# A graph network's GRU gates by block products: the state's side of the candidate as seven products, Silu as one function

## The chip, the cores and the metric

The kernel runs on one core of a Trainium2 chip. The metric is the time on the device in microseconds (us), the median of several runs. Everything is computed in fp32.

Five engines work side by side, each through its own instructions in order: TensorE (PE, with its weight loads shown as PEld), VectorE (DVE), ScalarE (ACT), GpSimd (POOL), and SyncE (SP), which issues DMA transfers. They wait for each other through semaphores. [...]

## The reference, cut to what matters

There are 128 graphs of 64 nodes with 256 features, and four layers, each with a residual and a layer norm. Layer 0 is a gated graph network of five steps, and most of the work lies there:

```python
A = (adj != 0).astype(x.dtype)
h = x
for l in range(weight.shape[0]):                 # five
    m = jnp.einsum('bnd,de->bne', h, weight[l])
    agg = jnp.einsum('bij,bid->bjd', A, m)
    h = _gru_cell(agg, h, w_ih, w_hh, b_ih, b_hh)

# _gru_cell(m, h, ...):
gi = m @ w_ih.T + b_ih                           # three gates of 256 columns
gh = h @ w_hh.T + b_hh
r = jax.nn.sigmoid(i_r + h_r)
z = jax.nn.sigmoid(i_z + h_z)
n = jnp.tanh(i_n + r * h_n)                      # n: the candidate; h_n: the state's side of it
return (1.0 - z) * n + z * h
```

Layer 1 is an MLP of 256 to 1024 to 256 on the aggregated nodes, with an RMS norm and `jax.nn.silu` between its two products. Layer 2 maps to and from a hyperbolic ball (a logarithm, a tanh), and layer 3 is attention over the graph's edges (an exp).

## The kernel before

Two graphs make a block of 128 rows, four blocks a group of 512 rows, and there are 16 groups. Three groups are in flight at a time, each with its own buffers. Features lie on the partitions: the state of a group is `h[128, 2, 512]`, two halves of the features (k) by 512 nodes, and the nodes are cut into two halves (n) of 256. The message weights are multiplied into the gate weights beforehand.

The kernel doesn't issue its instructions as they are written. It first records all operations with an assumed duration, then searches for an order of each engine by a beam search over that model, and issues them in that order. An operation that ScalarE or VectorE may do is given to one of them by the search. A PSUM bank is taken by the first operation on it and comes free after the last.

Gates r and z need `[r; z] = [[W_ar, W_hr], [W_az, W_hz]] [agg; h]`, a product of 2x2 blocks if the nodes are cut in two as well. Winograd's form of Strassen's scheme does such a product with seven block products and a few sums in place of eight. A block product here is 256x256 by 256x256, four matmuls of 128x128 by 128x256:

```python
def product(ps, w, v, first, last, r):
    for c in range(KD):                          # KD = 2
        for k in range(KD):
            pe(256, lambda c=c, k=k: nc.tensor.matmul(
                ps[:, c * HR:(c + 1) * HR], w[:, k, c * P:(c + 1) * P], v(k), ...))

def sides(n):                                    # aggregate, and the state's side of the candidate
    if l:
        ps = rows_of(h, n)                       # four transposes
        copied(512, ...)
    p_agg = aggregate(agg, hr, 2 * n, n)         # four matmuls of 128 columns, and a copy
    p_hn = bank("p_hn")
    product(p_hn, w_hn, lambda k: h[:, k, half(n)], True, True, (h, n))
    for c in range(KD):
        scaled(300, lambda c=c: hnb[:, c, half(n)], lambda c=c: p_hn[:, c * HR:(c + 1) * HR], lambda: 0.5, ...)
    return p_agg
# ... (cut)
sides(0)
product(p1, a11[l], k_of(a, 0), True, False, (a, 0))
copied(420, lambda: uu.tile(), lambda: blocks_of(p1.tile()), [uu], [p1])
product(p_in[0], w_in[l], k_of(a, 0), True, True, (a, 0))
product(p1, a12, k_of(h, 0), False, True, (h, 0))
tanh_half(ur, lambda c: p1[:, c * HR:(c + 1) * HR], 0, p1)
new_n(0, ur)
p_a2 = sides(1)
a2 = lambda: blocks_of(p_a2.tile())
minus(t1, a2, of(a, 0), [p_a2, (a, 0)])          # four VectorE sums of 512 columns
minus(t2, of(h, 1), lambda: view(t1), [(h, 1), t1])
minus(t3, of(h, 1), a2, [(h, 1), p_a2])
minus(t4, lambda: view(t2), of(h, 0), [t2, (h, 0)])
product(pu, s2[l], k_view(t2), True, True, t2)
plus(uu, pu, uu)
product(pv, s3[l], k_view(t3), True, False, t3)
plus(uv, pv, uu)
product(pw, s1[l], k_view(t1), True, False, t1)
product(pv, na22, k_view(t4), False, True, t4)
plus(uv, pw, uv)
plus(uz, pv, uu)
product(pw, s4[l], k_of(h, 1), False, True, (h, 1))
# ... (cut: the tanhs and the new state)
product(p_in[1], w_in[l], k_of(a, 1), True, True, (a, 1))
```

Sigmoids are computed as tanh of half the argument. The MLP's Silu is computed with tanh too, for each of eight chunks of 128 hidden features, with the missing 0.5 put into the residual and the RMS weight into `w2s` during the setup:

```python
dve(512, ... nc.vector.scalar_tensor_tensor(v, v, b1c(c), ps_r.tile(), OP.add, OP.mult) ...)
act(512, ... nc.scalar.activation(th.tile(), v, AF.Tanh, scale=half_r[:, c:c + 1]) ...)
dve(512, ... nc.vector.scalar_tensor_tensor(v, th.tile(), 1.0, v, OP.add, OP.mult) ...)
```

The MLP's first product is done in seven block products as well (`by_sums`, tiles `p_1h`, `p_uh`, `p_vh`, `p_wh`), except in the last two groups, where it is done directly (`ps_hid`). Its second product is `ps_o`.

Of the kernel before, what the change touches and what calls it, by code (L numbers as in the profile page):

```python
# [14 lines left out]
OP = mybir.AluOpType  # L15

P = 128
# [25 lines left out]
class Op:  # L43
    __slots__ = ("eng", "us", "run", "ways", "stream", "n", "kb", "need", "then", "bufs", "opens", "id", "way")

    def __init__(self, ways, stream, n, kb):
        self.ways = {eng: (us, run) for eng, us, run in ways}
        self.eng, self.us, self.run = ways[0]
        self.stream, self.n, self.kb = stream, n, kb
        self.need, self.then, self.bufs, self.opens, self.id, self.way = 0, [], (), None, 0, 0.0  # L50


class Plan:


    def __init__(self, flow):
# [10 lines left out]
        self.past, self.order = None, []  # L67

    def copy(self):
# [6 lines left out]
        c.past, c.order = (self.past, self.order), []  # L76
        return c

    def advance(self, until, rank):
# [3 lines left out]
        while self.left and clock["PE"] < until:  # L83
            best = None
            for s in range(self.first, min(self.first + flow.WINDOW, len(self.queues))):
                for e, q in self.queues[s].items():
                    opened = False
                    for _, o in zip(range(flow.AHEAD[e]), q):
# [10 lines left out]
                        key = (t + o.ways[e][0] - min(w[0] for w in o.ways.values()) if len(o.ways) > 1 else t, *rank(s, o))  # L99
# [4 lines left out]
            _, o, eng, t = best  # L104
            for e in o.ways:
                self.queues[o.stream][e].remove(o)
# [37 lines left out]
class Flow:  # L144
# [13 lines left out]
    HOPS = {"from PE": 0.25, "to PE": 0.3, "else": 0.1}  # L158
# [4 lines left out]
    WINDOW, STRETCH, WIDTH, LAG = 4, 25.0, 8, 40.0  # L163


    ENDGAME = 350.0
# [10 lines left out]
    def op(self, eng, us, run, w=(), r=(), kb=0):  # L177
        self.either([(eng, us, run)], w, r, kb)

    def either(self, ways, w, r, kb=0):  # L180

        o = Op(ways, len(self.streams) - 1, len(self.ops), kb)
# [31 lines left out]
    def hop(self, e, to):  # L214
        if e == to:
            return 0.0
# [14 lines left out]
    def issue(self):  # L231
        self.ways()
        ranks = (lambda s, o: (s, o.n), lambda s, o: (s if o.kb else -s, o.n), lambda s, o: (self.LAG * s - o.way, s, o.n))
        plans, until = [Plan(self)], 0.0
        while any(p.left for p in plans):
            late = until > self.work - self.ENDGAME
            until += self.STRETCH / 2 if late else self.STRETCH
# [6 lines left out]
            plans = [found[k] for k in sorted(found)[:self.WIDTH * (3 if late else 1)]]  # L244
# [16 lines left out]
def kernel(  # L261
# [79 lines left out]
    def dve(n, run, w, r):  # L341
        flow.op("DVE", 0.16 + 0.00105 * n, run, w, r)

    def act(n, run, w, r):
        flow.op("ACT", 0.27 + 0.00077 * n, run, w, r)

    def copied(n, o, i, w, r):

        flow.either([("ACT", 0.27 + 0.00077 * n, lambda: nc.scalar.copy(o(), i())),  # L349
                     ("DVE", 0.16 + 0.00105 * n, lambda: nc.vector.tensor_copy(o(), i()))], w, r)  # L350

    def scaled(n, o, i, scale, bias, w, r):

        flow.either([("ACT", 0.27 + 0.00077 * n, lambda: nc.scalar.activation(o(), i(), AF.Identity, bias=bias(), scale=scale())),  # L354
                     ("DVE", 0.16 + 0.00105 * n, lambda: nc.vector.tensor_scalar(o(), i(), scale(), bias(), OP.mult, OP.add))], w, r)
# [62 lines left out]
    def gate_w(name):  # L418
        return fixed([P, KD, D], name)

    a12, na22, w_hn = gate_w("a12"), gate_w("na22"), gate_w("w_hn")
    a11, s1, s2, s3, s4, w_in = ([gate_w(f"{n}_{l}") for l in range(L)] for n in ("a11", "s1", "s2", "s3", "s4", "w_in"))

# [5 lines left out]
    half_b, half_r = fixed([P, NV], "half_b"), fixed([P, KH], "half_r")  # L429
# [36 lines left out]
    flow.op("ACT", 1.5, lambda: nc.scalar.activation(warm, one4, AF.Tanh))  # L466
# [23 lines left out]
    dve(4, lambda: nc.vector.tensor_scalar(half_r.tile(), cols[:, 2 * NV + KH:], 0.5, None, OP.mult), [half_r], [cols])  # L490
# [13 lines left out]
    def hh_out(i, k, ps):  # L504
        if i == 0:
            dve(256, lambda: nc.vector.tensor_copy(a12[:, k, :], ps[:, :D]), [(a12, k)], [ps])
            dve(256, lambda: nc.vector.tensor_scalar(na22[:, k, :], ps[:, D:], -1.0, None, OP.mult), [(na22, k)], [ps])
        else:
# [594 lines left out]
```

## Time and profile before

| what | value |
|---|---|
| time, median of 3 runs | 2432.22 us (2432.07 to 2432.49) |
| span of the profiled execution | 2430.5 us |
| granted TensorE clock | 0.994 |
| bytes read from and written to HBM | 25.74 MB and 8.39 MB |

A group in the list of instructions reads: line of the kernel, engine, operation, output tile<-input tiles, shape, count; then after a bar the busy time in us and the mean duration of one in ns; then after another bar the idle time of that engine just before these instructions, with what ended it. A line can be that of a helper: all products of the GRU stand at one line and are told apart by their tiles. TensorE's records overlap, so that the busy times of its groups add up to more than its whole. A matmul of fp32 shows as two records, a transpose as one.

TensorE's waits over the whole span add up to little (engine, operation, what it waited for: us in total, times, longest):

```profile
PE ps_T L633 <- ACT x_n L354: 5.3, 1, 5.3
PE ps_sup L333 <- ACT tan L995: 3.6, 1, 3.6
PE ps_sup L333 <- DVE tan L994: 3.0, 1, 3.0
PE ps_hid L333 <- DVE aggm L350: 2.5, 1, 2.5
PE ps_x L469 <- POOL ident masks.py:199: 2.5, 1, 2.5
```

Four of these are of layers 1 to 3 of the last groups, and one is at the very start.

### The profile page before, as it was taken

What the parts mean: (1) busy time and instruction counts of PE and PEld (TensorE: products, weight loads), DVE (VectorE), ACT (ScalarE), POOL (GpSimd) and SP (SyncE); (2) the same over time, 40 slices, a digit from 0 to 9 for tenths busy, and PEclk for the clock granted to TensorE, in tenths of its full rate; (3) what the DMA queues carried; (4) which work ended last, traced back from release to release, by engine and by line L of the source; (5) the groups of instructions that cost most, each with busy time, mean ns of one, the idle gap of its engine ahead of it and who ended that gap; (6) DMA issues with size and microseconds to landing.
All of it is one profiled execution on the core that took longest, in us unless ns stands there. A gap on an engine that the chain in (4) does not pass through costs nothing.

```text
span 2430.5 us, 32703 instructions
## 1 busy us (share of the span) xinstructions
PE 2394.7 (99%) x12258; PEld 2102.9 (87%) x12258; DVE 1893.4 (78%) x4097; ACT 1147.1 (47%) x2408; POOL 188.2 (8%) x144
## 2 busy tenths in 40 slices
PE   9999999999999999999999999999999999999995
PEld 7888888888888888888888888888888888888864
DVE  3668787887888877778777887888787787878777
ACT  4434544444444444454444545455444544445453
POOL 4000000000100000000000100000000000000011
PEclk9999999999999999999999999999999999999997
DMA  4000000000000000000000000000000000000000
GB/s 127 3 1 12 1 29 1 18 12 1 29 1 27 3 18 11 1 27 3 16 14 1 29 1 27 3 19 11 1 29 1 18 12 1 27 9 18 9 9 18
DMA packets 39725, 36.21 MB, mean 15 GB/s; under 512 B 9956, under 2 KB 38656, under 8 KB 39568
## 3 DMA queue, kind: packets, MB, share of 16 engines
q1 hardware_dynamic: 37840, 32.25, 4.2%
q8 instruction: 97, 1.59, 0.3%
q10 hardware_dynamic: 1328, 1.31, 0.2%
q0 software_dynamic: 400, 0.57, 0.1%
q14 instruction: 60, 0.49, 0.1%
HBM read 25.74 MB, written 8.39 MB: 14 GB/s over the span
## 4 chain that ended last, share of the span: by engine, by line
PE 94%; DVE 4%; ACT 1%; DMA 1%; issue 0%; POOL 0%; SPq 0%; POOLq 0%; ACTq 0%; DVEq 0%
PE p_v L663 11%; PE p_w L663 11%; PE p_in L663 11%; PE p_r L663 11%; PE p_hn L663 11%; PE ps_o L333 9%; PE ps_agg L333 6%; PE p_u L663 6%; PE ps_hr L643 3%; PE ps_a L333 2%; PE p_wh L882 2%; PE p_vh L882 2%; PE p_1h L882 2%; PE ps_T L633 1%; PE ps_att L333 1%; PE p_uh L882 1%
## 5 line engine op out<-in xcount | busy, mean ns | idle before, releaser
L663 PE MATMUL p_hn<-hT,w_hn 128*128 128x256 f32 x1280 | 322.8, 380 | 0.0
L663 PE MATMUL p_in<-agg,w_in 128*128 128x256 f32 x1280 | 315.4, 379 | 0.0
L663 PEld LDWEIGHTS p_in<-agg,w_in 128*128 128x128 f32 x1280 | 240.2, 190 | 31.1
L663 PEld LDWEIGHTS p_hn<-hT,w_hn 128*128 128x128 f32 x1280 | 227.9, 191 | 22.7
L333 PE MATMUL ps_o<-w2s,hid 128*128 128x256 f32 x1024 | 231.2, 379 | 0.0
L333 PEld LDWEIGHTS ps_o<-w2s,hid 128*128 128x128 f32 x1024 | 193.9, 190 | 27.3 <-issue 1.2
L678 POOL TENSOR_TENSOR rstd<-ve,pow 128x4 f32<-128x4 f32 (+1 forms) x64 | 82.5, 1289 | 1491.6 <-DVE ve L676 1484.0
L767 ACT ACTIVATE V<-V,half_b 128x256 f32<-128x256 f32 x160 | 72.7, 500 | 199.2 <-DVE V L763 199.0
L663 PE MATMUL p_u<-tA,s 128*128 128x256 f32 x640 | 158.1, 381 | 1.4 <-DVE tA L746 0.6
L663 PE MATMUL p_w<-tA,s 128*128 128x256 f32 x640 | 158.1, 379 | 0.0
L663 PE MATMUL p_r<-hT,a 128*128 128x256 f32 x640 | 156.9, 379 | 0.0
L663 PE MATMUL p_r<-agg,a 128*128 128x256 f32 x640 | 156.7, 379 | 0.0
L663 PE MATMUL p_v<-tB,s 128*128 128x256 f32 x640 | 155.4, 379 | 0.0
L663 PE MATMUL p_v<-tB,na 128*128 128x256 f32 x640 | 154.5, 379 | 0.0
L663 PE MATMUL p_w<-hT,s 128*128 128x256 f32 x640 | 154.3, 379 | 0.0
L349 ACT COPY agg<-ps_agg 128x512 f32<-128x512 f32 x154 | 89.9, 584 | 114.2 <-PE ps_agg L333 98.8
L333 PEld LDWEIGHTS ps_agg<-edge,hr 128*128 128x128 f32 x1024 | 136.1, 191 | 6.6
L354 ACT ACTIVATE hnb<-p_hn,half_b 128x256 f32<-128x256 f32 x232 | 101.6, 472 | 81.4 <-PE p_hn L663 67.4
L333 PE MATMUL ps_agg<-edge,hr 128*128 128x128 f32 x1024 | 138.8, 275 | 0.0
L663 PEld LDWEIGHTS p_u<-tA,s 128*128 128x128 f32 x640 | 119.3, 190 | 21.0 <-DVE tA L746 2.3
L663 PEld LDWEIGHTS p_v<-tB,s 128*128 128x128 f32 x640 | 120.9, 190 | 16.3 <-PE ps_att L333 0.2
L663 PEld LDWEIGHTS p_w<-hT,s 128*128 128x128 f32 x640 | 120.7, 190 | 16.0
(233 smaller groups left out, 4686.5 us busy)
## 6 DMA issues: line engine op xcount, KB each, us to landing
x<-in_x_dram SPq DMA_DIRECT2D x16, 512.0 KB, 3.6
xr<-in_x_dram SPq DMA_DIRECT2D x16, 512.0 KB, 3.6
out_dram<-x_n SPq DMA_DIRECT2D x16, 512.0 KB, 2.9
edge<-in_adj_dram SPq DMA_DIRECT2D x32, 64.0 KB, 2.3
wm<-in_L_gnn_weight_dram SPq DMA_DIRECT2D x5, 256.0 KB, 5.3
w2s<-in_L_gnn_W_dram SPq DMA_DIRECT2D x1, 1024.0 KB, 10.0
w<-in_L_gnn_W_dram SPq DMA_DIRECT2D x2, 512.0 KB, 3.5
w_in_L_gnn_w_hh_dram<-in_L_gnn_w_hh_dram ACTq DMA_DIRECT2D x1, 512.0 KB, 5.2
```

The lines of the kernel that those rows point to most:

```text
L333: return nc.tensor.matmul(o, lhsT, rhs, start=(k == 0), stop=(k == nk - 1))
L349: flow.either([("ACT", 0.27 + 0.00077 * n, lambda: nc.scalar.copy(o(), i())), ("DVE", 0.16 + 0.00105 * n, lambda: nc.vector.tensor_copy(o( ...
L354: flow.either([("ACT", 0.27 + 0.00077 * n, lambda: nc.scalar.activation(o(), i(), AF.Identity, bias=bias(), scale=scale())), ("DVE", 0.16 ...
L633: turn(lambda j=j, c=c: nc.tensor.transpose(ps[:, c * HR + j * P:c * HR + (j + 1) * P], src[:, 2 * n + j, c * P:(c + 1) * P], ident.tile() ...
L643: turn(lambda j=j, c=c: nc.tensor.transpose(ps[:, j * D + c * P:j * D + (c + 1) * P], src[:, c, (2 * n + j) * P:(2 * n + j + 1) * P], iden ...
L663: pe(256, lambda c=c, k=k: nc.tensor.matmul(ps[:, c * HR:(c + 1) * HR], w[:, k, c * P:(c + 1) * P], v(k), start=first and c == k == 0, sto ...
L678: pool(1.1, lambda: nc.gpsimd.tensor_tensor(rstd[:, :m, :], ve[:, :m, :], pow2[:, :m, :], OP.pow), [rstd], [ve])
L767: act(256, lambda c=c: nc.scalar.activation(o[:, c, :], src(c), AF.Tanh, bias=half_b[:, i * KD + c:i * KD + c + 1], scale=0.5), [(o, c)], ...
L882: pe(256, lambda c=c: nc.tensor.matmul(ps[:, c * HR:(c + 1) * HR], w1f[:, w, (2 * q + c) * P:(2 * q + c + 1) * P], v[0](), start=first and ...
```

## The change

It has three parts that change what the engines do, and one that changes the search.

First, the gates are split in another way. The 2x2 blocks are no longer (aggregate, state) by (node halves), but (feature halves) by (node halves), once for the aggregate and once for the state. Both are summed in PSUM, so the chain of additions after the products stays one. The sums of the state (`tA`) then serve a second time.

Second, they serve the state's side of the candidate, which becomes a Winograd product of its own: seven block products of 128x128 by 128x256, one matmul each, in two banks.

Third, Silu is one ScalarE function, with the RMS weight as its scale; the second VectorE pass and the scaling of `w2s` go.

The search knows ScalarE's function tables (a change is taken to cost 1.28 us, and tanh is taken to be in the sets of both exp and silu), adds 0.4 us to VectorE's start where either engine may do an operation, has other assumed durations, and looks at more plans in smaller steps near the end. Each PSUM bank counts as one thing in it: an operation on one half of a bank comes after those before it on the other half if one of them writes.

The diff, cut to its core:

```diff
@@ the search
+                        elif o.sets and self.table not in o.sets:
+                            t += flow.TABLE
-                        key = (t + o.ways[e][0] - min(w[0] for w in o.ways.values()) if len(o.ways) > 1 else t, *rank(s, o))
+                        key = (t + flow.SOONER if len(o.ways) > 1 and e == "DVE" else t, *rank(s, o))
+    SOONER = 0.4
+    TABLE = 1.28
-    WINDOW, STRETCH, WIDTH, LAG = 4, 25.0, 8, 40.0
-    ENDGAME = 350.0
+    WINDOW, STRETCH, WIDTH, LAGS = 4, 37.5, 8, (60.0, 150.0,)
+    ENDGAME, LAST_STRETCH, LAST_WIDTH = 400.0, 10.0, 32
-            until += self.STRETCH / 2 if late else self.STRETCH
+            until += self.LAST_STRETCH if late else self.STRETCH
-            plans = [found[k] for k in sorted(found)[:self.WIDTH * (3 if late else 1)]]
+            plans = [found[k] for k in sorted(found)[:self.LAST_WIDTH if late else self.WIDTH]]
+    TANH, EXP, LN, SILU = ("exp", "silu"), ("exp",), ("ln",), ("silu",)
 ... (cut)
@@ the weights
-    a12, na22, w_hn = gate_w("a12"), gate_w("na22"), gate_w("w_hn")
-    a11, s1, s2, s3, s4, w_in = ([gate_w(f"{n}_{l}") for l in range(L)] for n in ("a11", "s1", "s2", "s3", "s4", "w_in"))
+    w_h, w_hn = fixed([P, 7, D], "w_h"), fixed([P, 7, P], "w_hn")
+    w_a, w_in = [fixed([P, 7, D], f"w_a_{l}") for l in range(L)], [fixed([P, KD, D], f"w_in_{l}") for l in range(L)]
-        sums("DVE", 0.7) if l == 0 else sums("POOL", 1.32)
+        sums_of(w_a[l], "DVE", 0.43) if l == 0 else sums_of(w_a[l], "POOL", 0.8)
-    for k in range(KH):
-        act(256, lambda k=k: nc.scalar.activation(w2s[:, k, :], w2s[:, k, :], AF.Identity, scale=rmsc(k)), [(w2s, k)], [(w2s, k), cols])
 ... (cut)
@@ the GRU
-                p_hn = bank("p_hn")
-                product(p_hn, w_hn, lambda k: h[:, k, half(n)], True, True, (h, n))
 ... (cut)
+            def sums(x, i):
 ... (cut)
+                for o, x0, x1 in ((of(t1), at(0, 1), at(0, 0)), (of(t2), at(1, 1), of(t1)),
+                                  (of(t3), at(1, 1), at(0, 1)), (of(t4), of(t2), at(1, 0))):
+                    dve(256, lambda o=o, x0=x0, x1=x1: nc.vector.tensor_sub(o[0](), x0[0](), x1[0]()),
+                        [o[1]], [x0[1], x1[1]])
 ... (cut)
+            def gate(ps, m, v, first, last):
+                for i, w in ((1, w_h), (0, w_a[l])):
+                    for c in range(KD):
+                        pe(256, lambda i=i, w=w, c=c: nc.tensor.matmul(
+                            ps[:, c * HR:(c + 1) * HR], w[:, m, c * P:(c + 1) * P], v[i][0](),
 ... (cut)
+            def state_side():
+                px, py = bank("p_hx"), bank("p_hy")
+                hs = u("hs", f"hs{l}", (P, 2, HR))
 ... (cut: prod is one matmul; plus is one VectorE addition of 256 columns out of PSUM)
+                prod(px, 0, m11, block(0, 0), True)
+                copied(256, su[0], lambda: px[:, :HR], [su[1]], [px])
+                prod(px, 0, m12, block(1, 0))
+                scaled(256, out(0, 0)[0], lambda: px[:, :HR], lambda: 1.0, lambda: b(0), [out(0, 0)[1]], [px, half_b])
+                prod(px, 1, ms2, sum_of(t2))
+                plus(su, px, 1, su)
+                prod(py, 0, ms3, sum_of(t3), True)
+                plus(sv, py, 0, su)
+                prod(py, 1, ms1, sum_of(t1))
+                prod(py, 0, mn22, sum_of(t4))
+                plus(out(0, 1), py, 0, su, 1)
+                plus(out(1, 1), py, 1, sv, 1)
+                prod(py, 1, ms4, block(1, 1))
+                plus(out(1, 0), py, 1, su, 0)
 ... (cut)
-            sides(0)
-            product(p1, a11[l], k_of(a, 0), True, False, (a, 0))
+            agg_of(0)
+            gate(p1, m11, block(0, 0), True, False)
             copied(420, lambda: uu.tile(), lambda: blocks_of(p1.tile()), [uu], [p1])
-            product(p_in[0], w_in[l], k_of(a, 0), True, True, (a, 0))
-            product(p1, a12, k_of(h, 0), False, True, (h, 0))
+            gate(p1, m12, block(1, 0), False, True)
             tanh_half(ur, lambda c: p1[:, c * HR:(c + 1) * HR], 0, p1)
+            sums(h, 1)
+            state_side()
+            product(p_in[0], w_in[l], lambda k: agg[:, k, half(0)], True, True, (agg, 0))
             new_n(0, ur)
-            p_a2 = sides(1)
 ... (cut: four minus lines go)
+            agg_of(1)
+            sums(agg, 0)
-            product(pu, s2[l], k_view(t2), True, True, t2)
+            gate(pu, ms2, sum_of(t2), True, True)
             plus(uu, pu, uu)
 ... (cut: pv, pw in the same way)
@@ the MLP's activation
-            act(512, lambda v=v, th=th, c=c: nc.scalar.activation(th.tile(), v, AF.Tanh, scale=half_r[:, c:c + 1]),
-                [th], [*parts, half_r])
-            dve(512, lambda v=v, th=th: nc.vector.scalar_tensor_tensor(
-                v, th.tile(), 1.0, v, OP.add, OP.mult), parts, [*parts, th])
+            act(512, lambda v=v, c=c: nc.scalar.activation(v, v, AF.Silu, scale=rmsc(c)), parts, [*parts, cols], SILU)
```

## The prediction

> **What bounds the kernel now.** I read the page's shares first, then TensorE's waits, then the stages, and only then the costs of single rows.
>
> ```profile
> PE 2394.7 (99%) x12258; PEld 2102.9 (87%) x12258; DVE 1893.4 (78%) x4097; ACT 1147.1 (47%) x2408; POOL 188.2 (8%) x144
> PE 94%; DVE 4%; ACT 1%; DMA 1%; issue 0%; POOL 0%; SPq 0%; POOLq 0%; ACTq 0%; DVEq 0%
> ```
>
> TensorE is busy for 2394.7 of 2430.5 us and makes up 94% of the chain that ended last; VectorE follows at 78%. [...] The stages say the same (columns: stretch, its length, then busy time and count of PE, PEld, DVE, ACT, POOL, the clock, DMA):
>
> ```profile
> 100.00:500.00 400.00, 399.53 (x2072) 354.51 (x2071) 311.21 (x640) 184.81 (x391) 19.49 (x15) 1.00 0.03 11
> 1000.00:1500.00 500.00, 500.00 (x2589) 444.50 (x2588) 401.10 (x886) 245.88 (x520) 34.84 (x24) 1.00 0.04 13
> 2300.00:2400.00 100.00, 86.38 (x350) 61.70 (x349) 77.28 (x192) 50.51 (x97) 13.86 (x9) 0.93 0.02 6
> 2400.00:2431.00 31.00, 14.61 (x64) 12.14 (x64) 22.17 (x86) 12.12 (x28) 4.72 (x4) 0.72 0.10 35
> ```
>
> In the middle TensorE stands still for nothing. Of its 35.8 us of idle time 13.6 + 16.4 = 30.0 lie after 2300 us, when the last groups run out of work for it, 3.4 in the first 30 us, and the rest, some 2.4 us, is spread over 2270 us. So one microsecond of TensorE work removed is one microsecond of time, as long as VectorE and the schedule keep up; anything removed elsewhere is worth nothing except in the last 50 us.
>
> **What one matmul costs.** Rows of the page can't be divided for this: a 128x256 fp32 product shows as two records of 379 ns that overlap with their neighbours (p_hn: 640 products in the code, x1280 in the row). I take a long unbroken run from the chain in order of time (start, length, what):
>
> ```profile
> 2363.80 15.99 PE ps_o L333 x74
> ...
> 2402.30 1.97 PE ps_T L633 x8
> ```
>
> 15.99 us / 74 records = 0.216 us for a record, 0.432 us for a product of 128x256. Check: all 256-wide records (7040 of the GRU, 1024 ps_o, 784 of the first MLP product, 552 others) make 9400 x 0.216 = 2030 us, 104 records of 512 columns make 45, and the 2754 transposes and 128-wide or narrower ones then have 320 us, 0.116 each, about half of 0.216. It closes, so there is no hidden cost for switching between streams.
>
> **The change part by part.**
>
> *Matmuls of the GRU.* Per group and layer the kernel before issues 44 products of 256 columns: 28 for the two gates r and z (p_r 8, p_u 4, p_v 8, p_w 8), 8 for p_in, 8 for the state's side p_hn (two halves x 2 x 2 blocks). After it the gates are split differently: the 2x2 blocks are no longer (aggregate, state) but the two feature halves, done once for the aggregate and once for the state, both summed in PSUM. That is 7 block products x 2 inputs x 2 output columns = 28 again. p_in keeps 8. The state's side of the candidate becomes one Winograd product of seven blocks, each one matmul: 7. So 43 in place of 44. Aggregations (8) and transposes (8) stay. Over 16 groups x 5 layers: 80 products x 0.432 = **34.6 us less for TensorE**. In the trace p_hn x1280 should become 1120 records, split over two tiles.
>
> *Sums on VectorE.* The rows before:
>
> ```profile
> L746 DVE TENSOR_TENSOR tA<-hT,tA 128x512 f32<-128x512 f32 x80 | 59.4, 742 | 1.4
> L746 DVE TENSOR_TENSOR tB<-tA,hT 128x512 f32<-128x512 f32 x80 | 57.9, 725 | 0.0
> L746 DVE TENSOR_TENSOR tA<-ps_agg,agg 128x512 f32<-128x512 f32 x80 | 54.9, 688 | 48.7 <-PE ps_agg L333 36.6 <-ACT agg L349 11.6
> L746 DVE TENSOR_TENSOR tB<-hT,ps_agg 128x512 f32<-128x512 f32 x80 | 54.5, 681 | 0.0
> L355 DVE TENSOR_SCALAR hnb<-p_hn,half_b 128x256 f32<-128x256 f32 x88 | 41.4, 480 | 19.6 <-PE p_hn L663 10.7 <-ACT hnb L354 8.5
> L878 DVE TENSOR_TENSOR t<-aggm 128x256 f32<-128x256 f32 x28 | 12.9, 462 | 1.8 <-ACT aggm L349 1.5
> L946 DVE SCALAR_TENSOR_TENSOR hid<-th,hid 128x512 f32<-128x512 f32 x128 | 82.8, 688 | 0.3 <-ACT th L944 0.2
> L354 ACT ACTIVATE hnb<-p_hn,half_b 128x256 f32<-128x256 f32 x232 | 101.6, 472 | 81.4 <-PE p_hn L663 67.4
> ```
>
> [...] Out go the four 512-wide sums, 59.4 + 57.9 + 54.9 + 54.5 = 226.7 us, the part of the scaling of p_hn that ran on VectorE, 41.4, and the second pass of the activation, 82.8: together 351. In come eight 256-wide sums for each group and layer, 640 x about 0.44 (the L878 rows, 462 down to 418 ns) = 281, and five 256-wide additions out of PSUM, 400 x 0.45 (the 128x256 operations that read PSUM lie between 420 and 484 ns) = 180. The copy and the scaling of the new chain, 160 in all, I leave mostly to ScalarE, since the new search delays VectorE by 0.4 us where either may do it; 15 us stay here, and some 20 us of other work move off by the same rule. Sum: 1893 - 351 + 281 + 180 + 15 - 20 = **about 2000 us, 83% of the span**, 85% in the middle against 80% now. [...] (0.69 to 0.74 us for 512 columns, 0.42 to 0.46 for 256, so about 0.15 of it is fixed), and that is why halving the width adds 54 us here. It stays below TensorE's 2360 and costs nothing by itself.
>
> *ScalarE.* 128 Tanh passes of 720 ns are replaced by 128 Silu passes of the same shape; I take the same duration. ScalarE loses 101.6 us of p_hn scaling and gains at most 160 x 0.45 = 72. What is new is the table: Tanh and Exp shared one table, and the only changes were to Ln and back:
>
> ```profile
> L975 ACT ACT_TABLE_LOAD x15 | 19.2, 1283 | 0.3
> L767 ACT ACT_TABLE_LOAD x10 | 12.8, 1283 | 0.2
> ```
>
> With the loads at three other lines that is 31, about two a group. [...] the change treats Silu as being in a set with tanh and without exp. Then a group needs Silu, Ln, and Exp or tanh, and with three groups mixed the order may go to and fro: I expect 45 to 65 loads, so 18 to 43 us more of ScalarE, at 47% load. Off the path, except that each holds up the operations behind it by 1.3 us.
>
> *Setup.* Eight scalings of w2s go (3.5 us of ScalarE), one half_r too; GpSimd's sums for layers 1 to 4 get smaller. TensorE does the same work there. Worth nothing, or a few tenths.
>
> *The end.* After the last ps_o, at 2379.8, there are 50.7 us of layer norm, logarithm, ball and attention. None of its operations changes; the search gets finer there (steps of 10 instead of 12.5 us, 32 plans instead of 24). I put the gain at 0 to 4 us, and a loss of 1 to 3 for an extra table load and longer layers of the last group. Net zero.
>
> *Sum.* TensorE work 2394.7 - 34.6 = 2360.1; idle time 35.8 + 2 for new short waits of TensorE in the middle = 37.8; with the 1.7 us between the profile's span and the time that is 2399.6; I take off 1.6 for the better end: **2398 us, 1.4% less**.
>
> **The rivals.**
>
> *The chain of the state's side becomes a wait.* The seven products hang together through two banks: product, eviction, product in the same bank, addition, and so on. [...] The chain is 7 x 0.43 + 7 x 0.46 = 6.2 us plus hand-overs, say 8 to 9, and it now needs both halves of the state. For it: r's candidate waits at its end, and two banks of eight are held three times as long. Against it: three groups are in flight, so each layer of a group, with some 22 us of TensorE work, has about 43 us of the other two to lie under, and the first MLP product already runs such chains (p_vh, p_uh) with 1.4 us of TensorE waiting in all. If it came true at 0.3 us for each layer, it would give back 24 us: about 2422.
>
> *VectorE becomes the bound in places.* At 85% in the middle, stretches with layer norms may go to 95%, and TensorE would wait for sums. Speaks against: now the share is 80% in each 500 us with next to no wait. Cost if true: 10 to 20 us, 2410 to 2415.
>
> *The end shrinks.* 30 us of idle time is there; if the finer search overlaps the last two groups better, 10 us may go, and the time would be 2386 to 2388. The evidence against it: the last group's own chain, from its last hidden product on, is serial, and nothing in it gets shorter but the activation.
>
> **Range and chances.** The saving in matmuls is counted, not guessed: 34.6 us, give or take one. What is uncertain is idle time: -10 at best, +15 to +20 if waits appear. So 8 in 10 lie in 2387 to 2412. Faster by over 2% means below 2383.6, with idle time cut from 36 to under 22: 0.08. Slower by over 2% would need 83 us of new waits: 0.02. Within 2%: 0.90.
>
> **What the profile would show.** TensorE busy near 2360 with 12258 - 160 = 12098 records; the state's products at 560 x 2 = 1120; idle before them below 10 us in all; VectorE near 2000 us; 45 to 65 table loads; no 512-wide sums and no second pass after the activation; idle time after the last 130 us near 30. I am wrong if TensorE's busy time doesn't fall by some 35 us (then products cost something by their order), if TensorE waits more than 10 us in the middle, or if the end is shorter or longer by more than 8.

## The result, and the profile after

The changed kernel takes 2416.41 us (median of 4 runs, 2414.99 to 2416.58) against 2432.35 us: a ratio of 0.9933 with a 95% interval of 0.9916 to 0.995. It is 16 us faster, not 34, and 18.4 us above the prediction. The prediction's range (2387 to 2412) doesn't hold it.

The page of the changed kernel: first the engines' busy time, then the chain that ended last.

```profile
PE 2364.1 (98%) x12098; PEld 2071.5 (86%) x12098; DVE 1894.3 (78%) x4404; ACT 1211.1 (50%) x2549; POOL 175.1 (7%) x144
...
PE 91%; DVE 6%; ACT 1%; issue 1%; POOL 0%; POOLq 0%; ACTq 0%; DVEq 0%
```

160 records of TensorE are gone, as counted. Its busy time fell by 30.6 us, and its idle time rose from 35.8 to 49.1 us. The stages tell where the idle time lies (stretch, length, then busy time and count of PE, PEld, DVE, ACT, POOL, the clock, DMA). The kernel before:

```profile
100.00:2300.00 2200.00, 2197.12 (x11373) 1950.59 (x11372) 1749.20 (x3729) 1044.79 (x2192) 143.42 (x99) 1.00 0.04 12
2300.00:2431.00 131.00, 101.00 (x414) 73.84 (x413) 99.45 (x277) 62.63 (x125) 18.58 (x13) 0.88 0.04 13
```

and the changed one:

```profile
100.00:2300.00 2200.00, 2188.26 (x11297) 1932.61 (x11296) 1764.17 (x4035) 1119.68 (x2355) 140.16 (x100) 1.00 0.04 12
2300.00:2414.00 114.00, 78.40 (x327) 59.56 (x325) 68.60 (x225) 55.26 (x112) 16.37 (x12) 0.85 0.04 15
```

Subtract the first busy time from the length. In the middle TensorE now stands still for 11.7 us where it stood 2.9. After 2300 us, with the spans of 2430.5 and 2413.2 us, it is 34.8 in place of 29.5 (the prediction has 30.0 there and 2.4 in the middle, since its last window ends 0.5 us after the span). The start gives 0.9 us back. So 30.6 - 8.8 - 5.3 + 0.9 = 17.4, and the spans differ by 17.3.

TensorE's waits in the middle of the changed kernel (for what: us in total, times, longest) name a tile that wasn't in the prediction's rivals:

```profile
PE ps_hr L655 <- DVE hT L847: 7.6, 8, 1.5
PE p_uh L938 <- DVE t L934: 1.9, 2, 1.0
PE p_v L772 <- DVE V L822: 0.5, 1, 0.5
PE p_hx L783 <- DVE hnb L366: 0.3, 1, 0.3
```

The transposes of the new state wait for VectorE's last operation on it, eight times for about 1 us. The seven products themselves (p_hx, p_hy) wait for almost nothing. At the end:

```profile
PE ps_T L645 <- ACT x_n L365: 10.2, 1, 10.2
PE ps_sup L342 <- ACT tan L1046: 5.9, 1, 5.9
PE ps_o L342 <- ACT hid L998: 4.8, 2, 4.5
```

These are the last groups' layer norm, logarithm and activation, waits of the kind that stood there before (5.3, 3.6 and 3.0 us), only longer.

**A measure that the busy time hides.** TensorE's records overlap: a record of 256 columns lasts 379 ns, but the next one starts 216 ns after it. A wait of up to 0.16 us is therefore counted as busy. I took all matmul records of a trace in order of their starts, and for each the distance to the next start, less the median distance of its shape. The medians times the counts give the work that the matmuls need: 2381.2 us before, 2346.7 after, so 34.5 us less. The excesses over 4 ns between 100 and 2300 us, summed, are what I call TensorE's lost time in the middle: **8.7 us before, 21.6 after.**

**One cause stands in the trace.** A stretch of the timeline around one of those eight waits (start, length, engine, operation, tiles):

```profile
1209.51 2.37 POOL L909 TENSOR_TENSOR xb<-x_n,b_r 128x1024 f32<-128x1024 f32 x1 [2.49 <-ACT x_n L365]
1210.27 2.16 DVE L845 SCALAR_TENSOR_TENSOR hT<-U,hT 128x512 f32<-128x512 f32 x1 [0.51 <-ACT U L826]
...
1212.46 0.69 DVE L847 SCALAR_TENSOR_TENSOR hT<-hT,R 128x512 f32<-128x512 f32 x1
...
1213.27 0.42 PEld L655 LDWEIGHTS ps_hr<-ident,hT 128*128 128x128 f32 x4 [1.34 <-PE p_1h L938]
1213.30 0.63 PE L655 MATMUL ps_hr<-ident,hT 128*128 128x128 f32 x4 [0.96 <-DVE hT L847]
```

The operation at L845 takes 2.16 us in place of 0.69: it reads two tiles of SBUF while GpSimd adds `xb`, once a group, 2.4 us long. It ends 0.55 us after GpSimd does. The operation behind it is late by the 1.5 us, and TensorE waits 0.96 us. In the whole middle of the changed kernel 15 VectorE operations are over 0.25 us longer than the median of their kind. All 15 lie beside `xb`, with 22.0 us in sum. Fourteen of them have two SBUF inputs; the fifteenth has one (a tensor_scalar of 64x256 on `edge`, 1.72 us in place of 0.29). None of the 15 reads PSUM; the operations that do, and that started within an `xb`, kept their length (`R<-p_in,R` 690 ns, its median 691; three `hnb<-p_hy` 476 to 484, median 476). The kernel before has 11, all beside `xb`, with 16.5 us. Of TensorE's lost time, 13.2 of 21.6 us fall within an `xb` or the 4 us after it, and 5.0 of 8.7 us before; these stretches are some 100 of 2200 us. So 8.2 of the 12.9 us by which the lost time grew lie there. The trace shows 1.47 us added to each in the mean, and not why. It is in both kernels; what changed is how much of it reaches TensorE. No run moved the `xb` addition to another engine, so its share is read from the trace and not tested. In each of the 20 traces of this case the VectorE operations that are so much too long, 8 to 15 of them, all lie beside `xb`. They don't explain the large differences between the runs below, though: at these places lie 8.8 of 64.7 us lost in e2, 8.5 of 52.1 in e4 and 16.5 of 58.2 in e17.

### The profile page after: what moved, and what is told of

Its sections match the earlier page's. It is cut to its first block, busy times and chain, and to the rows that moved or that the text cites. A ratio compares the mean times of both kernels' runs of the same rounds, so it can differ in the third digit from the quotient of the medians.

```text
span 2413.2 us, 32774 instructions
## 1 busy us (share of the span) xinstructions
PE 2364.1 (98%) x12098; PEld 2071.5 (86%) x12098; DVE 1894.3 (78%) x4404; ACT 1211.1 (50%) x2549; POOL 175.1 (7%) x144
## 4 chain that ended last, share of the span: by engine, by line
PE 91%; DVE 6%; ACT 1%; issue 1%; POOL 0%; POOLq 0%; ACTq 0%; DVEq 0%
PE p_v L772 11%; PE p_r L772 11%; PE p_w L772 11%; PE p_in L675 11%; PE ps_o L342 9%; PE ps_agg L342 6%; PE p_hy L783 6%; PE p_u L772 6%; PE p_hx L783 4%; PE ps_hr L655 3%; PE ps_a L342 2%; PE p_wh L938 2%; PE p_vh L938 2%; PE p_1h L938 2%; PE ps_sup L342 1%; PE ps_hid L342 1%
## 5 line engine op out<-in xcount | busy, mean ns | idle before, releaser
L772 PE MATMUL p_v<-tA,w_h 128*128 128x256 f32 x640 | 170.0, 379 | 0.5 <-DVE V L822 0.5
L772 PE MATMUL p_r<-hT,w_h 128*128 128x256 f32 x640 | 168.5, 379 | 0.0
L772 PE MATMUL p_v<-tB,w_a 128*128 128x256 f32 x640 | 167.1, 379 | 0.0
L772 PE MATMUL p_r<-agg,w_a 128*128 128x256 f32 x640 | 167.0, 380 | 0.0
L794 DVE SCALAR_TENSOR_TENSOR hnb<-p_hy,half_b,hs 128x256 f32<-128x256 f32 x240 | 108.6, 478 | 46.1 <-PE p_hy L783 45.2
L772 PEld LDWEIGHTS p_v<-tB,w_a 128*128 128x128 f32 x640 | 120.7, 190 | 16.1 <-DVE tB L759 0.2
L772 PEld LDWEIGHTS p_r<-agg,w_a 128*128 128x128 f32 x640 | 119.1, 190 | 15.9 <-issue 0.5
L772 PEld LDWEIGHTS p_v<-tA,w_h 128*128 128x128 f32 x640 | 118.4, 190 | 15.9 <-DVE V L822 1.4
L783 PE MATMUL p_hy<-tA,w_hn 128*128 128x256 f32 x480 | 131.3, 380 | 0.0
L772 PEld LDWEIGHTS p_r<-hT,w_h 128*128 128x128 f32 x640 | 116.6, 190 | 14.0 <-PE ps_hr L655 0.5
```

Of the source, the lines that this page charges most:

```text
L772: pe(256, lambda i=i, w=w, c=c: nc.tensor.matmul(ps[:, c * HR:(c + 1) * HR], w[:, m, c * P:(c + 1) * P], v[i][0](), start=first and i == 1 ...
L783: pe(256, lambda: nc.tensor.matmul(ps[:, j * HR:(j + 1) * HR], w_hn[:, m, :], v[1][0](), start=first, stop=True, skip_group_check=True), [ ...
L794: dve(300, lambda: nc.vector.scalar_tensor_tensor(o[0](), ps[:, j * HR:(j + 1) * HR], b(c), x[0](), OP.add, OP.add), [o[1]], [ps, x[1], ha ...
```

## The experiments

All times are medians, all ratios against the kernel before (its median was 2431.5 to 2432.1 us beside these runs). Lost time is the measure above; idle at the end is TensorE's after 2300 us.

| run | us | ratio, 95% interval | TensorE busy | lost in the middle | idle at the end |
|---|---|---|---|---|---|
| before | 2432.35 | | 2394.7 | 8.7 | 29.5 |
| changed | 2416.41 | 0.9916 to 0.995 | 2364.1 | 21.6 | 34.8 |
| e1 old state's side | 2445.71 | 1.0038 to 1.0072 | 2402.5 | 21.7 | 29.2 |
| e2 old Silu | 2462.65 | 1.0111 to 1.0142 | 2378.5 | 64.7 | 35.8 |
| e3 before, new search | 2451.14 | 1.0064 to 1.0094 | 2403.2 | 31.4 | 25.3 |
| e4 old durations | 2446.07 | 1.0044 to 1.0074 | 2378.6 | 52.1 | 29.1 |
| e5 old Silu, no chain | 2425.64 | 0.9967 to 0.9986 | 2371.0 | 29.4 | 32.9 |
| e6 no chain | 2426.67 | 0.997 to 0.999 | 2374.0 | 35.3 | 30.3 |
| e7 before, new durations | 2443.97 | 1.0036 to 1.0066 | 2397.9 | 15.3 | 35.5 |
| e8 before, new search, old durations | 2431.97 | 0.9994 to 1.0011 | 2397.3 | 12.5 | 25.3 |
| e9 before, ScalarE's durations | 2441.90 | 1.0026 to 1.0056 | 2397.2 | 16.6 | 28.7 |
| e10 before, VectorE's durations | 2441.21 | 1.0025 to 1.0054 | 2396.1 | 13.7 | 34.5 |
| e11 measured durations | 2443.42 | 1.0033 to 1.0063 | 2397.2 | 51.7 | 31.1 |
| e12 the same with margin | 2411.70 | 0.9903 to 0.9932 | 2374.9 | 20.7 | 29.0 |
| e13 and a longer hand-over | 2405.30 | 0.9877 to 0.991 | 2364.4 | 18.7 | 25.8 |
| e14 and a reordered chain | 2393.51 | 0.9829 to 0.9859 | 2359.5 | 10.3 | 22.1 |
| e15 reordered, more margin | 2409.15 | 0.9893 to 0.9923 | 2361.3 | 16.5 | 30.7 |
| e16 e14 without reordering | 2404.66 | 0.9875 to 0.9905 | 2361.8 | 12.7 | 31.2 |
| e17 reordering alone | 2456.46 | 1.0082 to 1.0116 | 2384.8 | 58.2 | 36.1 |
| e18 e14 with SOONER 0.2 | 2403.28 | 0.987 to 0.9899 | 2360.9 | 9.9 | 32.1 |

**Taking the change apart (e1 to e4).** My theory was that the seven products' chain gives the gain back. The rival was the search: the change shortens the durations that the search assumes, so its orders may be too tight.

e1, the state's side as two full products again:

```diff
-            state_side()                      # seven products, five additions
+            state_side(0)                     # p_hn: four products of 256 columns, two scalings
 ...
             sums(agg, 0)
+            state_side(1)
```

> The changed kernel with the state's side of the candidate as two full products again (44 products of 256 columns in place of 43), all else kept. TensorE's work rises by 80 x 0.432 = 34.6 us. If the missing gain is the seven products' own doing (a chain of additions, two banks held long), the waits of TensorE between 60 and 2290 us fall from some 20 to below 5 us, and the time is 2416 + 34.6 - 16 = about 2434 or less. If the new search and its shorter assumed durations make the orders too tight whatever the products are, the waits stay near 20 us and the time is about 2451. If it is Silu's tables, likewise about 2451.

2445.71. The lost time stays at 21.7 us. So it is not the seven products' own. They are worth 2445.71 - 2416.41 = 29.3 us of the 34.6; the rest lies at the end, where this run is idle for 29.2 us and the changed kernel for 34.8. What is left of the change without them is a loss of 13.6 us against the kernel before.

e2, Silu by tanh and two VectorE passes:

```diff
-            act(512, ... nc.scalar.activation(v, v, AF.Silu, scale=rmsc(c)) ...)
+            act(512, ... nc.scalar.activation(th.tile(), v, AF.Tanh, scale=half_r[:, c:c + 1]) ...)
+            dve(512, ... nc.vector.scalar_tensor_tensor(v, th.tile(), 1.0, v, OP.add, OP.mult) ...)
```

> The changed kernel with Silu by tanh and a second VectorE pass, as before. VectorE gets 83 us of work back, ScalarE loses some 15 table loads. If table loads make the waits, the time falls by some us, to about 2410. If VectorE's load is what lets the seven products' waits grow, waits in the middle rise to 40 us or more and the time to about 2440. If VectorE is merely busy in the shade of TensorE, as I had predicted, the time stays within 3 us of 2416.

2462.65, and the lost time triples. TensorE's three longest waits in the middle are for row operations of VectorE and ScalarE:

```profile
PE ps_o L342 <- DVE hid L1005: 7.4, 2, 7.1
PE ps_agg L342 <- ACT x_n L365: 6.9, 2, 5.3
PE ps_o L342 <- DVE y L1087: 3.6, 1, 3.6
```

The seven products wait for 5.5 of the 42.6 us that TensorE is idle in the middle. Table loads were not the trouble: this run has 31, the changed kernel 46. I had put Silu down as worth nothing outside the end.

e3, the kernel before with the whole new search (the two classes `Plan` and `Flow` and the assumed durations of the changed kernel; none of its activations names a table set).

> The kernel before with the whole new search (shorter assumed durations, ScalarE preferred, finer end), and no other change. If the shorter durations alone make TensorE wait, it gets slower by some 10 us, about 2442. If the seven products are the cause, its middle stays without waits; a better end could then make it about 2427.

2451.14: the search alone makes the kernel before **19 us slower**, all of it by waits (lost time 8.7 to 31.4), although the end gets 4 us shorter. The page shows less work on VectorE and more on ScalarE than before, and TensorE busier with the same matmuls:

```profile
PE 2403.2 (98%) x12258; PEld 2099.3 (86%) x12258; DVE 1803.4 (74%) x3844; ACT 1246.9 (51%) x2661; POOL 181.5 (7%) x144
```

e4, the changed kernel with the old, longer assumptions:

```diff
-        flow.op("DVE", 0.145 + 0.00105 * n, run, w, r)
+        flow.op("DVE", 0.16 + 0.00105 * n, run, w, r)
-        flow.op("ACT", 0.22 + 0.00077 * n, run, w, r, sets=sets)
+        flow.op("ACT", 0.27 + 0.00077 * n, run, w, r, sets=sets)
```

(and likewise where either engine may do it)

> The changed kernel with the kernel before's longer assumed durations for VectorE and ScalarE in the search (0.015 and 0.05 us more for each operation), nothing else. If too short durations make the waits, the waits in the middle fall to below 10 us and the time to about 2405. If the form of the state's side leaves no slack, longer durations only make the search leave idle time by itself, and the time rises, to 2425 or more.

2446.07. Longer assumptions alone don't mend it: lost time 52.1 us. Its waits are now partly those of the chain:

```profile
PE ps_hr L655 <- DVE hT L847: 12.4, 8, 4.3
PE p_hy L783 <- DVE tA L759: 4.1, 4, 1.4
PE p_hx L783 <- DVE tA L759: 3.2, 3, 1.9
```

So neither theory was whole. It looks as if the changed GRU finds orders without gaps only under short assumptions, which then make waits on the chip; but this is read from one order and not shown. e12, e13 and e16, which assume less than the change does for VectorE's independent operations and for copies and still lose less time, speak against it.

**The chain or VectorE's load (e5, e6).** Both take the chain apart. The seven products go into one PSUM bank (one of the kernel's eight, `BANKS = 8`, each a tile of 128x512 fp32) one after the other, and the copy and the scaling out of it and the five additions, now on SBUF tiles, follow. The count of instructions stays; the values of the candidate's state side are then not those of the reference.

```diff
-                px, py = bank("p_hx"), bank("p_hy")
+                px = bank("p_hx")
 ...                                         # all seven prod(px, ...) first, then:
-                plus(su, px, 1, su)
+                plus(su, out(0, 0), su)
```

e5 does it with the old Silu, so against e2:

> As the run with the old Silu (2462.65 us, VectorE's second pass back), but the chain of the state's side is taken apart: its seven products go one after the other into one bank, and the copy, the scaling and the five additions follow on what stands in SBUF. The same number of instructions on each engine; the candidate's state side is not what the reference asks. If VectorE's load makes TensorE wait, the time stays near 2462. If it is the chain and the second bank, TensorE's waits in the middle fall from 65 us to 25 or less, and the time to 2425 or less.

2425.64, 37 us less than e2, with VectorE a little busier (1972.0 us against 1962.8). So a load of this size doesn't by itself make a kernel as slow as e2. That it does so together with the chain and its second bank is one reading. The other is that the search merely came upon another order: e17 below keeps every operation, changes the order of the chain alone, and is 40 us slower.

e6 does it with the new Silu, so against the changed kernel:

> The changed kernel with the same chain taken apart (one bank, additions in SBUF). If the unplanned waits of the changed kernel (22 us in the middle) come from the chain, they fall below 10 us and the time to about 2404. If they come from the assumed durations and the choice of ScalarE in the search, they stay at about 20 us, and the time within 6 us of 2416.

2426.67: 10 us more than the changed kernel, lost time 35.3 us. With the new Silu nothing is gained by taking the chain apart, so the chain isn't shown to be what makes TensorE wait. What is left as a cause is the order and the assumptions that it comes from.

**Which part of the search (e7 to e10), on the kernel before.** e7 changes only the constants shown in e4, the other way round; e8 has the new search with the old constants; e9 and e10 change those of one engine.

> The kernel before with the new assumed durations of VectorE and ScalarE and nothing else of the new search. If short durations are what made the kernel before 19 us slower under the new search, this is near 2445 to 2451. If it was the rule that prefers ScalarE, this stays near 2432.

> The kernel before with the new search (ScalarE preferred by 0.4 us, larger steps, other ranks, finer end), but the old, longer durations. If the durations made it slower, this is near 2432 or a few us below by the better end. If the preference for ScalarE did, ScalarE is busier still than in the run with the whole new search (1247 us), and the time is near 2445 to 2451.

> The kernel before with ScalarE's new, shorter assumed durations alone (0.05 us less for each operation). Both engines' together made it 12 us slower (2443.97). If ScalarE's are to blame, this is near 2442; if VectorE's, near 2433; if neither alone but the order's accident, both of these two runs lie within 4 us of 2432.

> The kernel before with VectorE's new, shorter assumed durations alone (0.015 us less for each operation). If VectorE's are to blame, this is near 2442; if ScalarE's, near 2433.

e7: 2443.97. e8: 2431.97, the same as before. So the preference for ScalarE, the larger steps and the finer end cost nothing with the old durations (3.8 us more lost in the middle, 4.2 us less idle at the end); the durations alone cost 12 us. With both it is 19 (e3), so the parts don't add up. Nor do those of the durations: e9 (2441.90) and e10 (2441.21) are each near 2442, the mark that I had set for that engine alone being to blame, and both can't be. Each of these three is another order, and another order costs about 10 us here, part in the middle (13.7 to 16.6 us lost against 8.7) and, in e7 and e10, 5 to 6 us more at the end.

**Durations from the trace (e11 to e13).** In the changed kernel's trace, VectorE operations of 512 columns that follow each other at once start 0.61 us apart, or 0.725 where the second reads the first's result; ScalarE's copies of 512 columns from PSUM 0.48; its scalings of 256 columns with two column operands 0.49. The change assumed 0.683, 0.614 and 0.417, so its assumptions were not all too short.

```diff
-    HOPS = {"from PE": 0.25, "to PE": 0.3, "else": 0.1, "own": 0.0}
+    HOPS = {"from PE": 0.2, "to PE": 0.1, "else": 0.12, "own": 0.115}
-        flow.op("DVE", 0.145 + 0.00105 * n, run, w, r)
+        flow.op("DVE", 0.075 + 0.00105 * n, run, w, r)
-    SOONER = 0.4
+    SOONER = 0.2
 ...                                         # copies on ScalarE 0.08 + 0.00078 n, scalings 0.29 + 0.00077 n, a product 0.4325
```

> The changed kernel with assumed durations read from its own trace: starts of operations that follow each other at once on VectorE (512 columns 0.61 us, 0.725 where the second needs the first) and ScalarE (copy of 512 from PSUM 0.48, tanh of 256 0.41, scaling of 256 with two columns 0.49), TensorE 0.4325 us for a product, hand-overs to TensorE of 0.1 in place of 0.3 us; SOONER 0.2. If wrong assumptions are what costs the missing 18 us, the waits between 60 and 2290 us fall to 10 or less and the time to 2405 or less. If the seven products leave no slack on the chip whatever is assumed, the waits stay near 20 us and the time near 2416.

2443.42, a miss: both marks were lower, 2405 and 2416.

```profile
PE 2397.2 (98%) x12098; PEld 2048.0 (84%) x12098; DVE 1834.1 (75%) x4433; ACT 1203.9 (49%) x2520; POOL 173.0 (7%) x144
```

TensorE is "busy" 50 us longer than its matmuls need (2346.8). By the distances between starts, 526 waits of 0.17 us or less make up 34 of its 51.7 us of lost time; in the kernel before there are 98, of 4.0 us in all.

e12 adds 0.03 us to each VectorE and ScalarE operation, makes the hand-overs 0.115 and 0.135, and has SOONER 0.4. e13 then changes `"to PE": 0.115` to 0.3 and nothing else.

> As the run with the measured durations, but 0.03 us longer on VectorE and ScalarE, 0.015 longer hand-overs, SOONER 0.4. If short assumed durations make unplanned waits, this has fewer than the one without margin: below 8 us in the middle, and 2400 or less. If margins do nothing, both agree within 4 us.

> As the run with measured durations and a margin (2411.7 us), but the assumed hand-over to TensorE is 0.3 us again in place of 0.115, nothing else. That run had few waits of TensorE that show as idle (3 us in the middle), but TensorE was busy 28 us more than its matmuls need. If those are many short waits made by the short hand-over, TensorE's busy time falls from 2375 to 2365 or less; the order itself leaves some 9 us idle for it, so the time is about 2405 to 2410. If they are not, busy time stays at 2375 and the time rises to about 2420.

e12 is at 2411.70, 32 us below e11, with nearly the same hand-over (0.115 for 0.1), so e11's loss can't be put down to the short hand-over; its idle time in the middle is 3.2 us, but the 2400 us that went with it were missed. e13 is at 2405.30. The busy time shows what the longer hand-over did, 2374.9 us in e12 and here in e13:

```profile
PE 2364.4 (98%) x12098; PEld 2074.5 (86%) x12098; DVE 1819.6 (76%) x4423; ACT 1205.5 (50%) x2528; POOL 170.1 (7%) x144
```

10.5 us of short waits went, but 7.6 came back as plain idle time in the middle (lost time 18.7, from 20.7). Of the 6.4 us gained, 3.2 lie at the end.

**The chain's order (e14 to e18).** In each of its two banks the chain alternates three times between products and evictions. Two products into one bank, then two evictions, makes that two times, with the same sums:

```diff
                 prod(px, 0, m11, block(0, 0), True)
+                prod(px, 1, ms2, sum_of(t2))
                 copied(256, su[0], lambda: px[:, :HR], [su[1]], [px])
+                plus(su, px, 1, su)
                 prod(px, 0, m12, block(1, 0))
                 scaled(256, out(0, 0)[0], ...)
-                prod(px, 1, ms2, sum_of(t2))
-                plus(su, px, 1, su)
                 prod(py, 0, ms3, sum_of(t3), True)
-                plus(sv, py, 0, su)
                 prod(py, 1, ms1, sum_of(t1))
+                plus(sv, py, 0, su)
+                plus(out(1, 1), py, 1, sv, 1)
                 prod(py, 0, mn22, sum_of(t4))
+                prod(py, 1, ms4, block(1, 1))
                 plus(out(0, 1), py, 0, su, 1)
-                plus(out(1, 1), py, 1, sv, 1)
-                prod(py, 1, ms4, block(1, 1))
                 plus(out(1, 0), py, 1, su, 0)
```

e14 has this, e12's durations and a hand-over of 0.25; e15 has a margin of 0.04, 0.3 and SOONER 0.2; e16 is e14 without the reordering; e17 is the changed kernel with the reordering alone; e18 is e14 with SOONER 0.2.

> The changed kernel with the chain of the state's side put in another order, so that each of its two banks alternates twice with the evictions in place of three times (two products into a bank, two evictions, one or two products, evictions), the margin of 0.03 us, and a hand-over of 0.25. If the chain's banks are what leaves no slack, the order has none of the planned idle time and few short waits: 10 us or less in the middle, and 2395 to 2403. If the order of the chain does nothing, it is like the run with the hand-over of 0.3, 2405 to 2420.

> The same reordered chain with a margin of 0.04 us, a hand-over of 0.3 and SOONER 0.2. If the reordered chain gives slack that longer assumptions can use, fewer short waits than with 0.03 and 0.25: a time of 2395 to 2403. If longer assumptions only turn into planned idle time, 2405 or more.

> The best run (2393.5 us: reordered chain, margin 0.03, hand-over 0.25) with the chain in the changed kernel's own order again, nothing else. If the reordering is what gave the slack, the waits in the middle rise from 6 to 12 us or more and the time to 2402 or more. If the assumed durations were enough, the time stays within 4 us of 2393.5.

> The changed kernel with the reordered chain alone, under its own search settings. If the reordering alone gives slack, the time falls from 2416 to 2405 or less. If the short waits come from the assumptions whatever the chain's order, the waits in the middle are 20 us or more and the time is 2416 or more.

> The best run with ScalarE preferred by 0.2 us in place of 0.4: another order from nearly the same assumptions, for how much of a time is the order's accident. If the slack is real, the time lies within 6 us of 2393.5; if that run was a lucky order, it is at 2405 or more.

**e14 is the best of all, 2393.51 us, ratio 0.9844 (0.9829 to 0.9859), and beats both kernels.** Its page and stages:

```profile
PE 2359.5 (99%) x12098; PEld 2073.4 (87%) x12098; DVE 1830.6 (77%) x4441; ACT 1204.2 (50%) x2512; POOL 169.5 (7%) x144
```

```profile
100.00:2300.00 2200.00, 2193.39 (x11356) 1942.54 (x11354) 1718.44 (x4099) 1117.13 (x2329) 136.59 (x101) 1.00 0.04 12
2300.00:2392.00 92.00, 69.58 (x277) 53.22 (x277) 52.94 (x199) 50.71 (x102) 14.24 (x12) 0.85 0.04 12
```

The whole 34.6 us are there, and some more. But e18, the same with one constant of the search changed, is 10 us slower, at 2403.28, and e16, the same without the reordering, at 2404.66. The lost time of e14, e16 and e18 is 10.3, 12.7 and 9.9 us; what sets e14 apart is the end, 22.1 us idle in place of 31 to 32. That end is luck of the order: one constant of the search (e18) or the chain's order (e16) undoes it. The reordering is not shown to matter: e16 without it agrees with e18 within 1.4 us. Alone, under the change's own search, it makes the kernel 40 us slower (e17, 2456.46, lost time 58.2). So one order may differ from another by far more than 10 us with the same work.

The clean test of the search is e16 against the changed kernel: the operations are the same (who does those that either engine may do is the search's), only assumed durations and hand-overs differ, and it is 11.8 us faster. Its stages:

```profile
100.00:2300.00 2200.00, 2192.82 (x11344) 1939.48 (x11344) 1707.37 (x4049) 1124.65 (x2363) 141.96 (x101) 1.00 0.04 12
2300.00:2403.00 103.00, 71.71 (x282) 53.61 (x281) 57.03 (x213) 50.44 (x103) 13.74 (x11) 0.82 0.05 16
```

In the middle 8.9 us of lost time went (21.6 to 12.7), at the end 3.6 us of idle time. e13, whose operations are also the same, is 11.1 us faster, but mostly by its end (25.8 us idle for 34.8). All six orders with measured durations and a margin (e12 to e16, e18) lie at 2393.5 to 2411.7 us, below the two orders under the change's own settings (2416.41, and 2456.46 in e17); e15, whose assumptions are the longest of the six, is at 2409.15. That much is shown; which of the constants does it is not, since the gain lies now in the middle and now at the end.

## Why the prediction was wrong, step by step

- **Products, 34.6 us less: right.** 12098 records and 320 + 160 + 480 + 160 = 1120 of the state's side, as predicted. The work by the starts fell by 34.5 us. TensorE's busy time fell by 30.6 only, since 4 us of short waits count as busy.
- **VectorE's sums and additions: right in size.** They were estimated at 281 and 180 us. In the changed kernel the state's sums come to

```profile
L759 DVE TENSOR_TENSOR tA<-hT 128x256 f32<-128x256 f32 x160 | 69.3, 433 | 6.7 <-ACT hT L360 5.4
L759 DVE TENSOR_TENSOR tA<-hT,tA 128x256 f32<-128x256 f32 x80 | 33.8, 422 | 2.2
L759 DVE TENSOR_TENSOR tA<-tA,hT 128x256 f32<-128x256 f32 x80 | 33.3, 417 | 0.0
...
L794 DVE SCALAR_TENSOR_TENSOR hnb<-p_hy,half_b,hs 128x256 f32<-128x256 f32 x240 | 108.6, 478 | 46.1 <-PE p_hy L783 45.2
```

  136.4 us, those of the aggregate to 136.3, and the five additions to 108.6 + 33.8 + 33.5 = 175.9. VectorE's total of 2000 was off by 106 us all the same. I had let 20 us of free work move to ScalarE; about 100 moved, most likely by the rule that delays VectorE by 0.4 us: on the kernel before, the search with this rule and the old durations (e8) leaves VectorE 1803.9 us in place of 1893.4. Of the layer norms' 192 scalings 25 are left on it, from 114.
- **VectorE "stays below TensorE's 2360 and costs nothing by itself": not refuted, but too simple.** In e2 the old Silu's 83 us of VectorE work, not on the path by any sum, come with 46 us more. In e5 VectorE has as much to do, and 37 of them are gone. So what the work costs depends on the order that is found with it. Silu was the part of the change that I put at nothing, and in the one order found without it the rest is a loss.
- **ScalarE and tables: right.** 46 loads at 1283 ns (45 to 65 predicted), and Silu at 714 ns for Tanh's 720.
- **"Idle time 35.8 + 2 for new short waits", less 1.6 for a better end: the step that failed.** It was 49.1 us. Of the 18.4 us by which the time was missed, 12.9 are this (6.8 beyond the two in the middle, 6.9 at the end, with the 1.6 counted on, and 0.9 back at the start), 4.0 are the hidden waits in the busy time, and 1.5 the difference between the profiled run and the median. I knew that the durations in the search had changed, since I quote its rule on ScalarE, and took the order for given. e3, e7 and e8 show what I left out: on the kernel before, the whole new search costs 19 us, the new durations alone 12, and the rest of the search without them nothing. On the changed kernel's own operations, other assumed durations and hand-overs bring back 11 to 12 us (e13, e16) and so most of the 18.4. More than 10 us of waiting in the middle was among the signs of being wrong that I had named, and 11.7 came. Why the search's own order for the change waits where it does stays open, but for the 8.2 us beside `xb`.
- **The rival of the chain** (24 us, "two banks held three times as long") was the wrong cause for a right suspicion: the seven products wait for less than 1 us, and e1 without them loses as much. Taking the chain apart gains 37 us with the old Silu (e5 against e2) and loses 10 with the new one (e6 against the changed kernel). As the chain's reordering alone moves the time by 40 us (e17), neither shows that the chain itself is the reason, and no run takes it out under the longer assumptions of e4.
- **The end: wrong.** Predicted as zero, and as 1.6 us better in the sum, it cost 5.3 us. From 22 to 36 us in 20 traces, it goes by the order and hardly by the change.

## What to carry to other kernels

When a kernel's order is found by a search over assumed durations, a change of those durations is a change of the kernel like any other: run it alone on the old kernel, and run the new operations under several settings, before crediting the rest. A bound engine with next to no idle time doesn't say that there is slack: ask how the order comes about, and what longer operations elsewhere would do to it. And judge a small gain against the spread that orders of the same work have: here 10 us of 2400 between e14 and e18, which differ in one constant, and 40 between the changed kernel and e17.

## What the runs showed of the hardware

- Beside GpSimd's addition of 128x1024 from SBUF, single VectorE operations took longer, by 1.5 us in the mean (one of 128x512 2.16 us in place of 0.69). Between 100 and 2300 us this was so at 11 of the 14 additions before and at all 15 after, for one operation each. All of these operations but one have two SBUF inputs, and none reads PSUM. The search's model knows nothing of it, and 13.2 of the 21.6 us that TensorE lost in the middle of the changed kernel lie at these places.
- In the changed kernel, two VectorE operations of 512 fp32 columns with two tensor inputs and no column operand start 0.61 us apart when they are independent and about 0.72 when the second needs the first; 0.34 and 0.455 at 256 columns.
- TensorE's busy time hides short waits: 2397.2 us busy in e11 and 2359.5 in e14 are the same 12098 records. Distances between starts show them.
